# Inverses of the softmax sums: exp(-ln) on ScalarE and one Newton step on VectorE in place of VectorE's reciprocal

## The chip, the core and the metric

The kernel runs on one core of a Trainium2 chip. The metric is the device time of one execution in microseconds (us), the median of several runs. TensorE (PE) multiplies matrices, VectorE (DVE) and ScalarE (ACT) work elementwise, GpSimd (POOL) does masks, some sums and indirect DMAs, and SyncE (SP) issues most other DMAs. Each engine takes its instructions in a fixed order; between engines, semaphores say when a result is there.

## What is computed

Two transformer layers on a tensor of 8 batches of 512 tokens by 512 features, all in float32. Each of the four steps is followed by a layer norm:

```python
x = layernorm(x + attention0(x))     # 16 heads of 32, causal softmax
x = layernorm(x + experts(x))        # top 2 of 8 experts with low-rank adapters
x = layernorm(attention1(x))         # RMS-scaled input, 8 heads of 64, 2 key/value heads, adds x itself
x = layernorm(x + integer_ffn(x))    # weights given as integers and a scale for each row
```

In both attentions a head's output is softmax(scores) times the values. The kernel computes exp(scores) without subtracting a maximum, multiplies by the values, sums the exponentials of each query, and multiplies the product by the inverse of that sum. The change concerns this inverse.

## The kernel before

`usual_pass` runs four stages one after the other: attention 0 (0 to about 690 us), the expert tiles (to about 1060 us), attention 1 (to about 1600 us) and the integer FFN. A guard (`Guard`) gathers the sums of the exponentials and their inverses; if any were out of range, a slower general pass would follow.

**Attention 0** loops over 8 batches `b` and 4 groups `g` of four heads. A group has three units `u` of key tiles, `UNITS = ((0,), (1, 3), (2,))`. `scores` (L1477) lets TensorE fill `sc`, one tile that takes four banks of PSUM, and ScalarE takes the exponential (L1492) into `p`. Where `beside` holds, adapter products also go into `sc`, and ScalarE copies them out as `scaled` (L817) behind that exponential. GpSimd masks the diagonal (L1502). One unit later TensorE multiplies by the values (`av`, L1531), and VectorE adds up the `p` of a group (L1539). At the second unit of the next group, `normalise` (L1542) lets TensorE form the sums with a matrix of ones (`rs`, L1546). ScalarE copies them to `r_inv` and adds them up for the guard (L1081), VectorE takes the reciprocal (L1549) and multiplies (`aoT`, L1550). GpSimd adds the inverse to the guard's total (L1084). The other work of a batch (queries, keys, values, the output projection, the router, transposes `ps_x1T`) is put into slots of `plan` (L1563). TensorE follows the order in which this is written; the other engines' instructions are placed by the scheduler here, until the last groups.

**Attention 1** is written out by hand for TensorE, VectorE, ScalarE and GpSimd (`in_order`, L1805). A batch has 8 steps of two score units each; a group of two heads has four units, so two steps. In each step (L1966 to L1976) come, in order: the scores of two units (`sc`, two tiles of two banks) and their exponentials (L1876), VectorE's additions for the two units of the step before (`total`, L1884), the slot's other work, the products `av` (L1895) of the units of the step before, and every second step the normalisation of the group that is now complete (L1900): `rs` on TensorE (L1903), the copy on ScalarE (L1081), the reciprocal on VectorE (L1906), the product into `aoT` (L1913), and GpSimd's addition for the guard. The slots hold queries (`qT`, L1770), the key, the values, the projection `ps_o` of the batch before with its residual and statistics (L1848, L1856), and the preparation of the next batch (`xn`, L769; transposes L98). `r_inv` and `total` have one buffer each, `p` has four. PSUM outside the scores and `av` is two banks that `rs`, `ps_q`, `ps_k`, `ps_v` and `ps_o` take in turn.

ScalarE evaluates functions from a table that it has to load. Loads are put into the program when it is built. Before the change they stand at the first activation (L1404), around the router's exponential and the experts' Silu (L973, L526, L973), at the start of attention 1 (L1828, in `prepare_table(AF.Exp)`) and at its end (L1828, for Silu).

Of the kernel before, what the change touches and what calls it, by code (L numbers as in the profile page):

```python
# [9 lines left out]
F32 = mybir.dt.float32  # L10
# [3 lines left out]
AF = mybir.ActivationFunctionType  # L14
ALU = mybir.AluOpType
# [3 lines left out]
P = 128  # L19
NB = 8  # L20
S = 512
D = 512
NT = S // P
ND = D // P
# [26 lines left out]

SUM_LOW, SUM_HIGH = 1e-20, 1e20

WIDEST = 2048.0


# [11 lines left out]
def in_order(tc, *engines):  # L68


    return tc.manual_schedule(engines={mybir.EngineType.PE, *engines})


class Inputs:
# [40 lines left out]
class Env:  # L115
# [19 lines left out]
    def open_stream(self, ctx, batches, **kw):  # L135

        resident = ctx.enter_context(self.tc.tile_pool(name=f"resident{batches[0]}", bufs=1, **kw))
        for b in batches:
            self.xs[b] = resident.tile([P, NT, D], F32, tag=f"x{b}", name=f"x_{b}")
# [919 lines left out]
class Guard:  # L1059
# [26 lines left out]
    def partitions_held(self, const, ps):  # L1086
# [3 lines left out]
        nc.vector.tensor_reduce(red[:, 3:4], self.widest[:, : self.n_widest], AX.X, ALU.max)  # L1090
        nc.vector.tensor_scalar(red[:, 3:4], red[:, 3:4], WIDEST, None, ALU.is_le)
        nc.vector.tensor_reduce(red[:, 0:1], self.total, AX.X, ALU.add)
# [61 lines left out]
class IntegerFfn:  # L1154
# [102 lines left out]
    def batch(self, b):  # L1257
        env, nc = self.env, self.nc
        os = [self.p_o.tile([P, D], F32, tag=f"o{t}", name=f"ps_f{t}") for t in range(NT)]
        final = b == NB - 1  # L1260
        hold = NHID - self.HELD if final else NHID
        parts = {}
        for c in range(NHID):
            parts[c] = self.hidden(b, c, c >= hold)
            if 0 < c <= hold:
                for t in range(NT):
                    self.out(os, t, c - 1, parts[c - 1])

            if not final and c < NT:
                self.blocks(b + 1, c)  # L1270
            if not final and 0 <= c - 6 < ND:
                self.parts(b + 1, c - 6)
        if not final:
            for t in range(NT):
                self.out(os, t, NHID - 1, parts[NHID - 1])
            for t in range(NT):
                self.scaled(b, os, t)
            env.layernorm(b, lambda t: env.ins.out[b][ts(t, P), :])
            return

        with in_order(env.tc, mybir.EngineType.DVE, mybir.EngineType.Activation, mybir.EngineType.Pool):
            for t in range(NT):
                for c in range(hold, NHID):
                    self.out(os, t, c, parts[c])
                self.last_rows(b, t, self.scaled(b, os, t))
# [22 lines left out]
def attention0(env, guard, keep, routes, experts, dram, p_mm, tiles_ctx):  # L1308
# [4 lines left out]
    tc, nc, ins, xs, vec = env.tc, env.nc, env.ins, env.xs, env.vec  # L1313
    HD = 32
    scale = 1.0 / math.sqrt(HD)
    UNITS = ((0,), (1, 3), (2,))
    with ExitStack() as phase:
        work = phase.enter_context(tc.tile_pool(name="a_work", bufs=1))
# [4 lines left out]
        p_av = heads_ctx.enter_context(tc.tile_pool(name="a_av", bufs=2, space=PSUM))  # L1323


        wv, wq, wk, wo = (experts.room(i) for i in (0, 2, 3, 5))

        def load_w(room, i, units=slice(0, ND)):
# [45 lines left out]
        def mm(shape, name):  # L1374
            return p_mm.tile(shape, F32, tag="mm", name=name)
# [166 lines left out]
        def normalise(b, g, acc):  # L1542
            total, av = acc
            rs = p_av.tile([P, S], F32, tag="av", name="rs") if (b, g) == (NB - 1, ND - 1) else mm([P, S], "rs")
            for j in range(4):
                nc.tensor.matmul(rs[HD * j : HD * (j + 1), :], lhsT=ones, rhs=total[:, j, :], start=True, stop=True)  # L1546
            r_inv = work.tile([P, S], F32, tag="r_inv", name="r_inv", bufs=2)
            guard.watch_sums(rs, r_inv)
            nc.vector.reciprocal(r_inv, r_inv)  # L1549
            normed[0] = nc.vector.tensor_tensor(aoTs[b][:, g, :], av, r_inv, ALU.mult)  # L1550
            if (b, g) == (NB - 1, ND - 1):
                guard.watch_inverses(r_inv)
            else:
                inverses.append(r_inv)
# [65 lines left out]

        begun = phase.enter_context(ExitStack())
        begun.enter_context(in_order(tc))
        query(0, 0)
        key(0, 0)
        order = phase.enter_context(ExitStack())
        waiting = summing = None
        for b in range(NB):
            todo, late = plan(b)
            for g in range(ND):
                if g == (0 if b else 2) and b + 1 < NB:  # L1630
                    with behind_return():
                        load_xT(b + 1)
                if g == 3 and b + 1 < NB:
                    with behind_return():
                        load_x(b + 1)
                if b == NB // 2 and g == 0:
                    experts.load_lora(work, 1)
                if b == NB - 1 and g == 1:
                    experts.load(4)
                if b == NB - 1 and g == 2:  # L1640
                    order.enter_context(in_order(tc))
                if b == NB - 1 and g == 3:
                    experts.load(5)
                    experts.load(6)
                acc = []
                for u in range(len(UNITS)):
                    p = scores(b, g, u)
                    for thunk in todo[g, u]:
                        thunk()
                    begun.close()  # L1650
                    if waiting is not None:
                        waiting()
                    for thunk in late[g, u]:
                        thunk()
                    if u == 1 and summing is not None:
                        summing()
                    waiting = lambda b=b, g=g, u=u, p=p, acc=acc: product(b, g, u, p, acc)
                summing = lambda b=b, g=g, acc=acc: normalise(b, g, acc)
# [6 lines left out]
        b = NB - 1  # L1665
# [28 lines left out]
class Attention1:  # L1694
# [113 lines left out]
    def batches(self, work, p_sc, p_av, weights, split):  # L1808
        env, nc, guard, state, HD = self.env, self.nc, self.guard, self.state, self.HD
        xs = env.xs  # L1810
        scale = 1.0 / math.sqrt(HD)
# [14 lines left out]
        def prepare_table(function):  # L1826
            out = work.tile([P, 2, S], F32, tag="p", name="p1_none", bufs=4)
            nc.scalar.activation(out[:, 0, :1], env.neg_half[:, :1], function)  # L1828

        prepare_table(AF.Exp)  # L1830

        small = env.small
        pieces = {0: self.first}
# [35 lines left out]
        def score(b, g, kt):  # L1869
            st = state[b]  # L1870
            sc = p_sc.tile([P, 2, S], F32, tag="sc", name="sc1")
            for j in range(2):
                hs = slice(HD * j, HD * (j + 1))
                matmul_by_columns(nc, sc[:, j, :], st["kT"][hs, ts(kt, P)], st["qT"][g][hs, :], columns=HD)
            p = work.tile([P, 2, S], F32, tag="p", name="p1", bufs=4)
            nc.scalar.activation(p, sc, AF.Exp, scale=scale)  # L1876
            return p
# [10 lines left out]
        def product(b, g, kt, p):  # L1888
            st = state[b]
            if b and (g, kt) == (0, 0):  # L1890
                st["aoT"] = work.tile([P, ND, S], F32, tag="aoT", name="aoT1", bufs=2)
            if kt == 0:
                st["av"] = p_av.tile([P, S], F32, tag="av", name="av1")
            for j in range(2):
                nc.tensor.matmul(st["av"][HD * j : HD * (j + 1), :], lhsT=st["v"][:, kt, HD * j : HD * (j + 1)],  # L1895
                                 rhs=p[:, j, :], start=kt == 0, stop=kt == NT - 1)
            if kt == NT - 1:
                return lambda total=st["total"], av=st["av"]: normalise(b, g, total, av)

        def normalise(b, g, total, av):  # L1900
            rs = self.mm([P, S], "rs1")
            for j in range(2):
                nc.tensor.matmul(rs[HD * j : HD * (j + 1), :], lhsT=ones, rhs=total[:, j, :], start=True, stop=True)  # L1903
            r_inv = work.tile([P, S], F32, tag="r_inv", name="r_inv1")
            guard.watch_sums(rs, r_inv)
            nc.vector.reciprocal(r_inv, r_inv)  # L1906
            ao = state[b]["aoT"][:, g, :]
            if b != self.BY_TENSOR:

                ao, av, r_inv_ = self.turn.by_tile(ao, False), self.turn.by_tile(av, True), self.turn.by_tile(r_inv, True)  # L1910
            else:
                r_inv_ = r_inv
            nc.vector.tensor_tensor(ao, av, r_inv_, ALU.mult)  # L1913
            guard.watch_inverses(r_inv)
# [50 lines left out]
        for b in range(NB):  # L1965
            for i, thunks in enumerate(plan(b)):  # L1966
                units = [(b, u // NT, u % NT) for u in (2 * i, 2 * i + 1)]
                ps = [score(*unit) for unit in units]
# [4 lines left out]
                sums = [product(*unit) for unit in last]  # L1973
# [5 lines left out]
        sums = [product(*unit) for unit in last]  # L1979

        b = NB - 1
# [368 lines left out]
```

## Time and profile before

| | |
|---|---|
| median of 3 runs | 2098.43 us (2098.05 to 2098.45) |
| the profiled execution | 2098.14 us |
| its span, first to last instruction | 2096.2 us |
| mean granted TensorE clock | 0.999 |
| ScalarE copies of sums (L1081) | 64, mean 597 ns |
| reciprocals, attention 0 (L1549) | 32, 107.0 us |
| reciprocals, attention 1 (L1906) | 32, 107.1 us |
| table loads seen on ScalarE | 6, mean 1283 ns |

In the profile, a line such as `L1906 DVE RECIPROCAL r_inv<-r_inv ... x32 | 107.1, 3347 | 72.7 <-ACT r_inv L1081 72.7` names the line of code, the engine, the operation, output and input, how many, the busy us, the mean ns of one, then the idle us of the engine just before them and who ended it. A row of a time line has the start in us, the duration in us, engine, line, operation and count; in square brackets stands the idle time before it and who ended it. PEld is the loading of weights into TensorE. The ends of matmuls are modelled, and a busy TensorE is not necessarily one at its peak.

### The profile page before, as it was taken

What the parts mean: (1) busy time and instruction counts of PE and PEld (TensorE: products, weight loads), DVE (VectorE), ACT (ScalarE), POOL (GpSimd) and SP (SyncE); (2) the same over time, 40 slices, a digit from 0 to 9 for tenths busy, and PEclk for the clock granted to TensorE, in tenths of its full rate; (3) what the DMA queues carried; (4) which work ended last, traced back from release to release, by engine and by line L of the source; (5) the groups of instructions that cost most, each with busy time, mean ns of one, the idle gap of its engine ahead of it and who ended that gap; (6) DMA issues with size and microseconds to landing.
All of it is one profiled execution on the core that took longest, in us unless ns stands there. A gap on an engine that the chain in (4) does not pass through costs nothing. (4 is left out here: it accounts for less than half of the span.)

```text
span 2096.2 us, 35861 instructions
## 1 busy us (share of the span) xinstructions
PE 2072.5 (99%) x15074; PEld 1048.4 (50%) x15074; DVE 1275.9 (61%) x1965; ACT 606.8 (29%) x840; POOL 503.3 (24%) x509
## 2 busy tenths in 40 slices
PE   9999999999999999999999999999999999999998
PEld 2333333333334677774433333333335888888886
DVE  2667776777768633234157888887868644455444
ACT  2333433324333111111143333333332322222222
POOL 1343444434433221221052231222101000000000
PEclk9999999999999999999999999999999999999999
DMA  9011304324233568876431332233102311111000
GB/s 327 22 46 57 102 16 117 122 70 154 82 102 112 171 200 256 243 225 203 148 101 51 121 111 81 66 106 101 41 1 71 101 41 61 61 61 61 20 21 22
DMA packets 182090, 213.39 MB, mean 102 GB/s; under 512 B 72586, under 2 KB 126090, under 8 KB 178850
## 3 DMA queue, kind: packets, MB, share of 16 engines
q1 hardware_dynamic: 169280, 172.85, 26.3%
q0 software_dynamic: 10560, 34.61, 5.7%
q10 hardware_dynamic: 2082, 3.56, 0.6%
q8 instruction: 121, 1.98, 0.4%
q14 instruction: 47, 0.39, 0.1%
HBM read 132.58 MB, written 78.40 MB: 101 GB/s over the span
## 5 line engine op out<-in xcount | busy, mean ns | idle before, releaser
L1492 ACT ACTIVATE p<-sc 128x2048 f32<-128x2048 f32 (+1 forms) x96 | 153.1, 1595 | 172.0 <-PE sc L65 148.3
L1236 DVE SCALAR_TENSOR_TENSOR hT<-ps_u,vec,sg 128x512 f32<-128x512 f32 x88 | 65.5, 745 | 190.1 <-PE ps_u L1231 189.9
L1084 POOL TENSOR_TENSOR g_total<-g_total,r_inv 128x512 f32<-128x512 f32 x64 | 90.7, 1417 | 351.8 <-DVE r_inv L1906 270.8
L1247 PE MATMUL ps_f<-ffn_w,h_half 128*128 128x512 f32 x664 | 167.7, 393 | 2.7 <-DVE h_half L1242 2.0
L964 PE MATMUL ps_gu<-xrT,experts 128*128 128x256 f32 x736 | 166.6, 379 | 0.0
L964 PEld LDWEIGHTS ps_gu<-xrT,experts 128*128 128x128 f32 x736 | 139.3, 190 | 35.9 <-issue 19.3
L1539 DVE TENSOR_TENSOR p<-p 128x1536 f32<-128x1536 f32 (+2 forms) x96 | 136.5, 1422 | 32.6 <-PE av L1531 17.6
L1502 POOL TENSOR_SCALAR_AFFINE_SELECT p<-p 128x512 f32<-128x512 f32 x128 | 84.4, 672 | 290.7 <-ACT p L1492 287.6
L1876 ACT ACTIVATE p<-sc 128x1024 f32<-128x1024 f32 x128 | 124.2, 1022 | 100.3 <-PE sc L65 99.0
L1906 DVE RECIPROCAL r_inv<-r_inv 128x512 f32<-128x512 f32 x32 | 107.1, 3347 | 72.7 <-ACT r_inv L1081 72.7
L1247 PEld LDWEIGHTS ps_f<-ffn_w,h_half 128*128 128x128 f32 x664 | 122.9, 188 | 34.4 <-DVE h_half L1242 7.3
L1231 PE MATMUL ps_g<-x_high,ffn_w 128*128 128x512 f32 x352 | 137.2, 390 | 0.0
L1231 PE MATMUL ps_g<-x_low,ffn_w 128*128 128x512 f32 x352 | 137.0, 389 | 0.0
L1231 PE MATMUL ps_u<-x_high,ffn_w 128*128 128x512 f32 x352 | 137.0, 389 | 0.0
L1231 PE MATMUL ps_u<-x_low,ffn_w 128*128 128x512 f32 x352 | 137.0, 389 | 0.0
L65 PE MATMUL sc<-qT,kT 64*64 64x512 f32 x1024 | 124.7, 602 | 1.2 <-ACT qT L1770 0.9
L65 PE MATMUL ps_q<-experts 128*32 128x512 f32 x1024 | 121.2, 602 | 4.7 <-DMA experts<-in_xT 4.4
L65 PE MATMUL ps_v<-experts 128*32 128x512 f32 x1024 | 120.9, 594 | 0.0
L1895 PE MATMUL av<-p,v 128*64 128x512 f32 x512 | 120.8, 593 | 0.0
L1234 ACT ACTIVATE sg<-ps_g,vec 128x512 f32<-128x512 f32 x88 | 60.6, 689 | 195.4 <-PE ps_g L1231 195.4
L65 PE MATMUL ps_o<-attn_out,aoT 128*64 128x512 f32 x512 | 116.4, 598 | 0.0
L65 PE MATMUL ps_k<-experts 128*32 128x512 f32 x1024 | 116.3, 594 | 0.0
(280 smaller groups left out, 3270.3 us busy)
## 6 DMA issues: line engine op xcount, KB each, us to landing
results<-y SPq DMA_DIRECT2D x68, 256.0 KB, 2.9
pair<-xrT SPq DMA_DIRECT2D x30, 512.0 KB, 3.0
xrT<-pair SPq DMA_DIRECT2D x120, 128.0 KB, 3.9
turned<-turned SPq DMA_DIRECT2D x56, 256.0 KB, 4.1
x<-in_x SPq DMA_DIRECT2D x8, 1024.0 KB, 8.5
rows<-x SPq DMA_DIRECT2D x32, 256.0 KB, 2.1
experts<-in_xT SPq DMA_DIRECT2D x7, 1024.0 KB, 11.8
x<-rows SPq DMA_DIRECT2D x14, 512.0 KB, 6.6
```

Of the source, the lines that this page charges most:

```text
L65: nc.tensor.matmul(out[m], lhsT=lhsT[:, m], rhs=rhs, start=start, stop=stop)
L964: nc.tensor.matmul(ps[:, j, :], lhsT=w, rhs=xT[:, c, :], start=c == 0, stop=c == ND - 1)
L1084: self.nc.gpsimd.tensor_tensor(self.total, self.total, r_inv, ALU.add)
L1231: nc.tensor.matmul(ps, lhsT=w[:, ts(dc, P)], rhs=x[:, dc, :], start=(dc, i) == (0, 0), stop=(dc, i) == (ND - 1, 1))
L1236: nc.vector.scalar_tensor_tensor(hT, u, vec[:, V_SU + c : V_SU + c + 1], sg, ALU.mult, ALU.mult)
L1247: self.nc.tensor.matmul(os[t], lhsT=h[:, ts(t, P)], rhs=self.weights(2 * NHID + c), start=(c, i) == (0, 0), stop=(c, i) == (NHID - 1, 1))
L1492: nc.scalar.activation(p, sc[:, :, :width], AF.Exp, scale=scale)
L1502: select = nc.gpsimd.affine_select(out=first, in_=first, pattern=[[0, 4], [1, P]], compare_op=ALU.is_ge, fill=0.0, base=0, channel_multipl ...
L1539: nc.vector.tensor_tensor(total[:, :, P * kt :], total[:, :, P * kt :], p[:, :, at : at + w], ALU.add)
L1876: nc.scalar.activation(p, sc, AF.Exp, scale=scale)
L1895: nc.tensor.matmul(st["av"][HD * j : HD * (j + 1), :], lhsT=st["v"][:, kt, HD * j : HD * (j + 1)], rhs=p[:, j, :], start=kt == 0, stop=kt ...
L1906: nc.vector.reciprocal(r_inv, r_inv)
```

## The change

Of the 64 inverses, 63 are made by a new function; the last one of attention 0 keeps its reciprocal. ScalarE takes ln of the sums straight from PSUM, then exp of minus that; VectorE makes one Newton step of it, with `sums` the copy that the guard's line makes: (2 - sums * rough) * rough. In attention 0 `rough` takes a buffer of the tag `r_inv`, which has two; in attention 1 it has one of its own. At the start of attention 0 and of attention 1 a table set that holds both functions is asked for; in attention 1 this stands in place of the activation that prepared Exp.

```diff
+EXP_AND_LN = "natural_log_exp_and_others"
...
+def inverse(nc, sums, ps, rough):
+
+    nc.scalar.activation(rough, ps, AF.Ln)
+    nc.scalar.activation(rough, rough, AF.Exp, scale=-1.0)
+    nc.vector.scalar_tensor_tensor(sums, sums, -1.0, rough, ALU.mult, ALU.mult)
+    nc.vector.scalar_tensor_tensor(sums, sums, 2.0, rough, ALU.add, ALU.mult)
...
+        nc.scalar.preload_act_table_set(EXP_AND_LN)
         wv, wq, wk, wo = (experts.room(i) for i in (0, 2, 3, 5))
...
             guard.watch_sums(rs, r_inv)
-            nc.vector.reciprocal(r_inv, r_inv)
+            if (b, g) == (NB - 1, ND - 1):
+                nc.vector.reciprocal(r_inv, r_inv)
+            else:
+                inverse(nc, r_inv, rs, work.tile([P, S], F32, tag="r_inv", name="r_rough", bufs=2))
...
-        prepare_table(AF.Exp)
+        nc.scalar.preload_act_table_set(EXP_AND_LN)
...
             guard.watch_sums(rs, r_inv)
-            nc.vector.reciprocal(r_inv, r_inv)
+            inverse(nc, r_inv, rs, work.tile([P, S], F32, tag="r_rough", name="r_rough1"))
```

In the changed kernel's numbering the preloads are L1336 and L1844, Ln and Exp of the inverse L78 and L79.

## Prediction, made before the changed kernel was run

> **What bounds the kernel now.** I read the page's busy shares first, then the waits of TensorE in the two stretches that hold the attentions, then time lines around a normalisation. The page:
>
> ```profile
> PE 2072.5 (99%) x15074; PEld 1048.4 (50%) x15074; DVE 1275.9 (61%) x1965; ACT 606.8 (29%) x840; POOL 503.3 (24%) x509
> ...
> L1906 DVE RECIPROCAL r_inv<-r_inv 128x512 f32<-128x512 f32 x32 | 107.1, 3347 | 72.7 <-ACT r_inv L1081 72.7
> ```
>
> TensorE is busy for all but 23.7 us of the span. 64 reciprocals cost VectorE 214 us, but VectorE is not what the span is made of. Waits of TensorE in 40 to 700 us (attention 0); each row is us in total, times, longest:
>
> ```profile
> PE sc L65 <- ACT p L1492: 1.2, 1, 1.2
> PE ps_x1T L1443 <- DVE r_table L603: 0.7, 1, 0.7
> ```
>
> And in 1055 to 1610 us (attention 1), the longest:
>
> ```profile
> PE sc L65 <- ACT qT L1770: 0.9, 1, 0.9
> ```
>
> All of TensorE's waits in attention 0 come to 2.8 us, in attention 1 to 3.4. So the gain is capped at some 6 us even if every wait there vanished, and most are not behind a reciprocal. What matters is the slack of the new chain. The place to read is a normalisation in attention 1 and the next row sum (time line of a middle batch, VectorE, TensorE and weight loads):
>
> ```profile
> 1189.65 1.89 PE L1895 MATMUL av<-p,v 128*64 128x512 f32 x8
> ...
> 1190.93 0.14 PEld L1903 LDWEIGHTS rs<-total,ones 128*64 128x64 f32 x2 [0.28 <-issue]
> ...
> 1193.22 3.35 DVE L1906 RECIPROCAL r_inv<-r_inv 128x512 f32<-128x512 f32 x1 [5.44 <-ACT r_inv L1081]
> ...
> 1196.68 0.69 DVE L1913 TENSOR_TENSOR aoT<-av,r_inv 128x512 f32<-128x512 f32 x1
> ...
> 1197.28 1.73 DVE L1884 TENSOR_TENSOR total<-p,p 128x1024 f32<-128x1024 f32 x1
> ...
> 1203.71 2.52 DVE L1884 TENSOR_TENSOR total<-total,p 128x1024 f32<-128x1024 f32 x2
> ...
> 1204.86 1.89 PE L1895 MATMUL av<-p,v 128*64 128x512 f32 x8
> ...
> 1206.35 0.38 PEld L1903 LDWEIGHTS rs<-total,ones 128*64 128x64 f32 x4 [0.48 <-issue]
> 1206.58 1.03 PE L1903 MATMUL rs<-total,ones 128*64 128x512 f32 x4
> ```
>
> The first reciprocal begins only when ScalarE's copy of the sums ends (VectorE had sat idle 5.44 us), and from its end VectorE works without a gap to 1206.23, when the next group's total is ready. The next row sum loads its weights 0.12 us later, 1.49 us after its av began, where the undisturbed distance is 1.28 (1189.65 to 1190.93). So that total is already just in time: TensorE has no slack there, though no wait is printed. The same place recurs every 67.8 us.
>
> **What the change removes and adds.** Per inverse it removes a 3.35 us reciprocal and adds on VectorE two scalar_tensor_tensor of 128x512. Nearest row: L735, 741 ns, in pairs 1.53 us; L1254's plain two-operand form at 684 is the lower end. I take 1.53. On ScalarE it adds Ln and Exp of 128x512, nearest row L1081, 597 ns. Saved on VectorE 1.8 us, 63 times, 115 us; added on ScalarE 1.2 us, 76 us. Both engines have room, so neither sum is a time.
>
> The instruction order of the built program shows more. TensorE, GpSimd and SyncE keep their orders; no DMA moves. In attention 0 ScalarE has one table load at its start (L1336) and none before the expert tiles. In attention 1 the preload of L1844 leaves no instruction. A load stands before the first score exp (where L1828's stood) and **one ahead of every Ln and one ahead of every Exp of the inverse, 64 in all**. What one costs, from ScalarE's time line in the expert tiles:
>
> ```profile
> 721.21 0.60 ACT L973 ACTIVATE h<-ps_gu 128x512 f32<-128x512 f32 x1 [2.98 <-PE ps_gu L964]
> 721.83 1.28 ACT L526 ACT_TABLE_LOAD   x1
> 723.12 0.23 ACT L526 ACTIVATE tmp<-tmp 128x32 f32<-128x32 f32 x1
> ```
>
> End of one activation to start of the next: 1.31 us, nothing hidden around the load. The Trainium skill, "ScalarE: Activation LUTs", section "What ACT_TABLE_LOAD costs", gives about 1283 ns for the load, which agrees, and adds about 1380 ns of drain, 2.66 us for every switch. It speaks against this change; the row shows no drain, and I take 1.31. By the page the chain below would be 2.7 us longer (first rival). Its section "Table sets" says Ln and Exp share a set and need one load; the built program in attention 1 does not do that.
>
> **Attention 1.** From the end of ScalarE's copy, C: before, reciprocal at C+0.04, 3.35, 0.11 to the product, 0.69: aoT done at C+4.19. After: load 1.31, Ln 0.60, load 1.31, Exp 0.60 = C+3.82, two vector steps with their gaps 1.69, product 0.69: C+6.2. So **aoT is 2.0 us later; I take 1.95**, with 1.8 to 2.0 from the two vector prices. Queued behind the waiting vector step are aoT, the next adds, residuals and statistics; behind ScalarE's chain the two score exps of the next step. VectorE's saving can't pay this back where VectorE was waiting for the copy anyway.
>
> Against it, place by place (end of the last add to the weight load of the row sum, less 0.12 latency, plus what a late weight load hides, about 0.2):
> - Normalisation in a batch's first step, next total (1138, 1206, 1274, 1342, 1410, 1477 us): slack nil. 6 x 1.95 = 11.7.
> - The next one: VectorE reaches the reciprocal 1.7 us after the copy, so C+3.82 exceeds its arrival by only about 2.1 while 1.8 of work are saved: 0.35 late, slack 0.33. Nothing.
> - The third (five batches): slack 1.25-0.12+0.2 = 1.34. 5 x 0.6 = 3.0.
> - The fourth: slack 6.3. Nothing.
> - Batch 0: row sum at 1086.47, its total ended 1086.42: 1.95. Transposes at 1096.54, xn ended 1096.44: 1.9.
> - Batch 7: slack 1.7 at 1574.88: 0.25. Slack 0.3 at 1587.21: 1.65.
> - Entry of the integer FFN: its first matmul at 1599.81 follows the third residual (ended 1599.76); VectorE is then 1.3 later than TensorE: 1.3.
>
> Sum 21.8. The score exps come 3.8 us later: at 1261 the first ends at 1265.8 instead of 1262.3, its bank is wanted at 1267.29, 1.5 us spare. The qT copies of batch 0 end some 0.2 late, inside the waits already counted. The final aoT comes at 1595.6, its matmuls at 1596.2.
>
> **Attention 0.** No loads, so the chain is C+1.2+1.7+0.69 against 4.19: shorter, and VectorE is often behind anyway. ScalarE's third exp of a group slips by about 0.75 us. Where logits follow, the bank is close:
>
> ```profile
> 331.93 1.08 ACT L817 ACTIVATE scaled<-sc 128x512 f32<-128x512 f32 x2
> ...
> 333.53 1.11 PE L65 MATMUL sc<-q,k 32*64 32x512 f32 x16
> ```
>
> scaled would end at 333.75 instead of 333.01: 0.3 us, 6 batches, 1.8. In other groups the bank is wanted over 1 us after. Of the 0.7 us wait for r_table at 644, which lies behind a reciprocal, I credit all: -0.7. Bounds -2.8 to +4; I take +1.1.
>
> **Sum.** 21.8 + 1.1 = 22.9 on the profiled execution's 2098.14 us (span 2096.2 and 1.9 around it): 2121.0. The median of the runs is 0.29 higher: 2121.3.
>
> **The rivals.**
> 1. The load costs 2.66 us as the page says. aoT is then 4.65 late; places 1 to 3 of a batch cost 4.65, 2.7 and 3.3, batch 0 9.3, the end 12: about 83 us, 2181. Against it: the time line above. 5 in 100.
> 2. VectorE's lateness shrinks on its way. The first add after aoT takes 1.73 us beside GpSimd's g_total, the same shape later 1.26; if that add falls free and the vector steps take 684 ns, the delay is about 1.3: 6 x 1.3, 0 for the third place, 2.6 in batch 0, 1.6 at the end, and attention 0 gives 0.5 back: 2110. For it: the two durations; against: g_total starts when r_inv is ready, so it moves along. 14 in 100.
> 3. **Not slower:** ScalarE loads a table while still waiting or computing, so that loads stay off the chain. The chain is C+3.6, 0.6 shorter than now; only the capped wait remains to be won: 2097.5. It decides where a load costs under some 0.34 us on the chain (1.31 less half of 1.95). Against it: Ln's load stands after the copy that waits, in order, and the row shows 1.31 between activations. 7 in 100. That the change doesn't do what it says is shown in part already by the 64 loads.
> 4. The score exps also stall TensorE: if the chain exceeds the 1.5 us spare by 0.5 in half the groups, 8 us more: 2132. 6 in 100.
>
> **How the numbers follow.** The likeliest case has 68 in 100 and its own range 2114 to 2128 (delay 1.8 to 2.05, attention 0 from -2 to +4). The range reaches to rivals 2 and 4: 2108 to 2133, some 83 in 100. About 0.2%, 4 us, is what a measurement of this kernel tells from no change. Slower: cases 1, 2, 4 and the likeliest, 0.92; within 0.2% 0.06; faster 0.02, since the cap is 6 us.
>
> **What would show it.** In attention 1 two table loads of 1.28 us per inverse, aoT about 6.2 us after the copy's end; TensorE waits of about 1.95 us at rs <- DVE total, six times, and 0.6 five times; GpSimd waiting longer for r_inv. In attention 0 no loads, VectorE's busy time down by 57 us. The span should grow in 1060 to 1610 and hardly in 40 to 700. It is wrong if a load has a gap around it, if rs shows no wait, or if attention 0 grows by over 4 us.

## The result, and the profile after

The changed kernel takes 2121.14 us (median of 4 runs, 2120.95 to 2121.2), the kernel before beside it 2098.44 (2098.05 to 2098.79): ratio 1.0108, 95% interval 1.0091 to 1.0126. It is 22.7 us slower. The profiled execution has a span of 2119.4 us, 23.2 more than before.

The page after, busy times and the first vector step of the inverse:

```profile
PE 2078.7 (98%) x15074; PEld 1048.2 (49%) x15074; DVE 1170.3 (55%) x2028; ACT 753.4 (36%) x1029; POOL 507.3 (24%) x509
...
L80 DVE SCALAR_TENSOR_TENSOR r_inv<-r_inv,r_rough 128x512 f32<-128x512 f32 x63 | 44.0, 698 | 160.2 <-ACT r_rough L79 160.0
```

VectorE is busy 105.6 us less than before, and yet the kernel is slower. At 47 of the 63 inverses VectorE now sits idle until ScalarE's `r_rough` is there, 160 us in all; before, it sat idle 72.7 us for the copies of the sums. TensorE's longest waits in 1055 to 1640 us (us in total, times, longest):

```profile
PE rs L1917 <- DVE total L1898: 15.8, 13, 2.5
PE ps_g L1241 <- DVE x L1862: 1.0, 1, 1.0
```

Neither row stands in the list of before. The time line of the place that the prediction showed (a batch's first normalisation, ScalarE and VectorE, and the next row sum):

```profile
1201.47 0.60 ACT L1091 ACTIVATE r_inv<-rs 128x512 f32<-128x512 f32 x1 [2.05 <-PE rs L1917]
1201.97 0.19 ACT L1091 ACTIVATION_READ_ACCUMULATOR r_inv<-rs 128x1 f32 x1
1202.18 1.28 ACT L78 ACT_TABLE_LOAD   x1
1203.47 0.60 ACT L78 ACTIVATE r_rough<-rs 128x512 f32<-128x512 f32 x1
1204.09 1.28 ACT L79 ACT_TABLE_LOAD   x1
1205.38 0.63 ACT L79 ACTIVATE r_rough<-r_rough 128x512 f32<-128x512 f32 x1
1205.92 1.92 ACT L1890 ACTIVATE p<-sc 128x1024 f32<-128x1024 f32 x2
...
1206.12 0.69 DVE L80 SCALAR_TENSOR_TENSOR r_inv<-r_inv,r_rough 128x512 f32<-128x512 f32 x1 [6.23 <-ACT r_rough L79]
...
1207.64 0.69 DVE L1927 TENSOR_TENSOR aoT<-av,r_inv 128x512 f32<-128x512 f32 x1
...
1208.25 1.79 DVE L1898 TENSOR_TENSOR total<-p,p 128x1024 f32<-128x1024 f32 x1
...
1217.40 1.08 PE L1917 MATMUL rs<-total,ones 128*64 128x512 f32 x4 [1.68 <-DVE total L1898]
```

The copy ends, with its accumulator read, at 1202.16; `aoT` is done at 1208.33, 6.17 us later (4.19 before). From `aoT` on VectorE has no gap until the next total, and the row sum, just in time before, now waits 1.68 us.

To see where the time came from, I set the start of each group of TensorE's products in the profile after against the start of the same group before. The shift grows in the steps below. Steps of up to 0.1 us are left out, and so is one of 0.76 us at 74.86 us, which is gone again at the next group.

| place (time before) | step, us |
|---|---|
| keys' first product, 9.65 us | 1.20 |
| six score groups behind logits, 165 to 586 us | 6 x 0.21 |
| `ps_x1T` at 645.88, first scores of attention 1 at 1061.47 | -0.18, -0.18 |
| batch 0: `rs` at 1086.47, scores at 1087.48, `ps_q` at 1089.36 | 2.65, 0.25, 1.39 |
| `rs` at 1138.79 and every 67.8 us, six times | 1.85 to 1.86 each |
| `rs` at 1172.65 and every 67.8 us, five times | 0.52 to 0.53 each |
| `rs` at 1575.31 and 1587.64, entry of the integer FFN at 1599.81 | 0.14, 1.55, 1.04 |

About 21 us arise in attention 1, about 2 before it. The theory to test: the two table loads on each chain make VectorE late, and the adds queued behind that wait make the row sum late. Rivals: attention 0 carries a good part; the added activations and vector steps cost by themselves; the loads hold up the score exponentials; a load costs more than its 1.28 us.

### The profile page after: what moved, and what is told of

It reads as the page before. It is cut to its first block, busy times and chain, and to the rows that moved or that the text cites. A ratio compares the mean times of both kernels' runs of the same rounds, so it can differ in the third digit from the quotient of the medians.

```text
span 2119.4 us, 36153 instructions
## 1 busy us (share of the span) xinstructions
PE 2078.7 (98%) x15074; PEld 1048.2 (49%) x15074; DVE 1170.3 (55%) x2028; ACT 753.4 (36%) x1029; POOL 507.3 (24%) x509
## 5 line engine op out<-in xcount | busy, mean ns | idle before, releaser
L1513 POOL TENSOR_SCALAR_AFFINE_SELECT p<-p 128x512 f32<-128x512 f32 x128 | 98.6, 782 | 339.6 <-ACT p L1503 337.0
L1550 DVE TENSOR_TENSOR p<-p 128x1536 f32<-128x1536 f32 (+2 forms) x96 | 144.3, 1503 | 37.5 <-POOL x L1523 31.4
L80 DVE SCALAR_TENSOR_TENSOR r_inv<-r_inv,r_rough 128x512 f32<-128x512 f32 x63 | 44.0, 698 | 160.2 <-ACT r_rough L79 160.0
L1091 ACT ACTIVATE r_inv<-rs 128x512 f32<-128x512 f32 x64 | 38.2, 597 | 244.2 <-PE rs L1917 119.7
```

The source lines that it names most:

```text
L1513: select = nc.gpsimd.affine_select(out=first, in_=first, pattern=[[0, 4], [1, P]], compare_op=ALU.is_ge, fill=0.0, base=0, channel_multipl ...
L1550: nc.vector.tensor_tensor(total[:, :, P * kt :], total[:, :, P * kt :], p[:, :, at : at + w], ALU.add)
```

## Experiments: which attention, and which part of the chain

**Attention 0 alone.** Attention 1 as before (`prepare_table(AF.Exp)`, `nc.vector.reciprocal`).

> Only attention 0 takes the new inverse; attention 1 keeps VectorE's reciprocal and its own preparation of Exp. My theory: nothing in attention 0 loads a table, the inverse is off TensorE's path, and only ScalarE's later third exponentials reach TensorE where logits follow (6 x 0.21 us in the trace after), against some 0.35 gained at waits; with the 1.2 us that the trace after shows at its first key product, if that belongs to the table load asked for at the start, 2100.5 us; without it 2099.3. Rival, that the two extra ScalarE activations and the changed order in attention 0 cost a good part of the 22.7 us: over 2105.

2099.32 us; before 2098.24; ratio 1.0006 (0.9997 to 1.0015). The six steps of 0.21 us are there. But the keys' first product starts 0.44 us *earlier* than before, with the same early load.

**Attention 1 alone.** Attention 0 as before.

> Only attention 1 takes the new inverse, with its 64 table loads; attention 0 is as before. My theory: all of the loss but some 2 us lies here, by an aoT that comes 1.9 to 2 us late: 2119.5 us (2118.5 to 2121). Rival, that attention 0 carries a good part of it: under 2115.

2119.65 us, ratio 1.0103 (1.0087 to 1.0118): 21.4 of the 22.7 us. The trace also shows where attention 1's request for the shared set went. L1840 is that request's line in this kernel:

```profile
1.25 1.28 ACT L1840 ACT_TABLE_LOAD   x1 [1.25 <-PEq L2350]
```

It was carried out 1.25 us after the program's start, some 1060 us before attention 1. Before attention 1 begins, three other loads follow it, for the router and the experts (at 667.96, 721.50 and 729.31 us). In the full change the load at 1.25 us stands at attention 0's request, and none is seen at attention 1's.

**One set.** The whole change with one line kept:

```diff
+        prepare_table(AF.Exp)
         nc.scalar.preload_act_table_set(EXP_AND_LN)
```

> The whole change, but in attention 1 the activation that prepares Exp stays and the shared set is asked for after it: in the built program the shared set is then loaded once there, and the 64 loads before Ln and Exp are gone; nothing else in the inverse differs. My theory (the loads make the chain late): the chain is 3.6 us from the copy's end to aoT instead of 6.2 (4.2 before), TensorE never waits for it, and what is left is attention 0's: 2099.5 us (2098 to 2100.5). Rival, that Ln, Exp and the two vector steps themselves, or ScalarE's fuller queue, are what costs: over 2110.

2100.22 us, ratio 1.0007 (0.9998 to 1.0016). The same place in its time line:

```profile
1195.87 0.19 ACT L1091 ACTIVATION_READ_ACCUMULATOR r_inv<-rs 128x1 f32 x1
1195.96 0.59 ACT L78 ACTIVATE r_rough<-rs 128x512 f32<-128x512 f32 x1
1196.58 0.63 ACT L79 ACTIVATE r_rough<-r_rough 128x512 f32<-128x512 f32 x1
...
1198.84 0.69 DVE L1928 TENSOR_TENSOR aoT<-av,r_inv 128x512 f32<-128x512 f32 x1
```

With one load of the shared set ahead of the stage (its group has one entry, 1.3 us), `aoT` is done 3.47 us after the copy, and none of the steps at 1138 to 1478 us is left; of batch 0's steps 0.42 us remain. The 21 us are the 64 loads, not Ln, Exp or the Newton step.

**One set, attention 1 alone.** As above, attention 0 as before.

> As the run before, but attention 0 as before the change. My theory: attention 1 can only win what it waits for, 3.4 us at most, and hardly any of these waits is behind a reciprocal: 2097.5 us (2096 to 2098.5), a little faster than the kernel before or the same. Rival as in the run before: over 2108.

2099.10 us, ratio 1.0004 (0.9995 to 1.0013): not the small gain that I thought likely. A chain 0.7 us shorter than the reciprocal's wins nothing, since TensorE's longest waits in the stage are the same as before (`sc` on `qT` 0.9, `ps_hT` 0.7), and none is behind an inverse. One short wait is even new: 0.3 us at batch 0's row sum. There the first inverse's two vector steps took 0.98 and 1.06 us, with GpSimd at work beside them, instead of 0.69 each.

**Loads kept, Newton step left out.** In this run and in all the others below, up to the gathers behind, attention 0 is as before the change.

```diff
-            inverse(nc, r_inv, rs, ...)
+            r_inv = work.tile([P, S], F32, tag="r_rough", name="r_rough1")
+            nc.scalar.activation(r_inv, rs, AF.Ln)
+            nc.scalar.activation(r_inv, r_inv, AF.Exp, scale=-1.0)
```

> Attention 1 alone, with its 64 table loads, but the Newton step is left out: exp(-ln) itself is multiplied with av. aoT then ends at the copy's end + 3.85 + 0.04 + 0.69 = 4.6 us instead of 6.2 (before: 4.2). My theory (what counts is by how much aoT is late): 0.4 late, six places of a batch's first step 6 x 0.3, batch 0 and the end 0.3 to 0.5 each, the third place nothing: 2101.5 us (2100 to 2104). Rival (each load costs by itself, some 0.3 us for each of 64): 2117 or more.

2099.95 us against 2098.70, ratio 1.0005 (0.9996 to 1.0015), just under the range that I expected. There are six steps of 0.26 us at the six places and nothing elsewhere in attention 1, not in batch 0 and not at the end either. With sixty-four loads the loss is about 1.3 us, and the interval holds none at all: what counts is by how much the chain is longer than before (4.57 us from copy to `aoT` instead of 4.19), not how many loads there are.

**Copies in the loads' place.** The shared set is loaded once, as in the one-set runs.

```diff
     nc.scalar.activation(rough, ps, AF.Ln)
+    for _ in range(4):
+        nc.scalar.activation(rough, rough, AF.Copy)
     nc.scalar.activation(rough, rough, AF.Exp, scale=-1.0)
```

> Attention 1 alone with the shared set, so no loads, but four copies of rough to itself (ScalarE, 128x512, about 0.62 us each with the gap) between Ln and Exp: 2.5 us in the place of the 2.6 that two loads took. My theory (a load costs as any other work of its length on this chain): nearly the same time as with the loads, 2118.5 us (2116.5 to 2120). Rival (there is something about table loads, such as a drain or their fetch, beyond their 1.28 us): under 2110.

2119.40 us, ratio 1.0096 (1.0079 to 1.0112). Its longest wait of TensorE:

```profile
PE rs L1916 <- DVE total L1897: 15.5, 13, 2.6
```

This is the pattern of the loads without the loads: 13 waits, steps of 1.80 at the six places (1.85 with loads), 0.47 at four of the five and 0.76 at the other. On this chain a load costs what any other 1.28 us of ScalarE would.

**Loads behind the chain.** Shared set, and two needless loads after each Exp.

```diff
     nc.scalar.activation(rough, rough, AF.Exp, scale=-1.0)
+    nc.scalar.preload_act_table_set("exp_and_others")
+    nc.scalar.preload_act_table_set(EXP_AND_LN)
```

> Attention 1 alone with the shared set, and behind each inverse's Exp two loads that nothing needs (Exp's own set, then the shared one again): 64 loads as in the changed kernel, but behind the chain to aoT and ahead of the next step's score exponentials. My theory (VectorE's lateness is what costs, the score exponentials have 1.5 us to spare): 2099.5 us (2098.5 to 2102). Rival (the loads hold up the score exponentials and through them TensorE): over 2110.

```profile
1193.22 0.19 ACT L1093 ACTIVATION_READ_ACCUMULATOR r_inv<-rs 128x1 f32 x1
...
1193.94 0.63 ACT L79 ACTIVATE r_rough<-r_rough 128x512 f32<-128x512 f32 x1
1194.59 1.28 ACT L80 ACT_TABLE_LOAD   x1
1194.68 0.69 DVE L82 SCALAR_TENSOR_TENSOR r_inv<-r_inv,r_rough 128x512 f32<-128x512 f32 x1 [7.45 <-ACT r_rough L79]
...
1195.87 1.28 ACT L81 ACT_TABLE_LOAD   x1
1196.20 0.69 DVE L1926 TENSOR_TENSOR aoT<-av,r_inv 128x512 f32<-128x512 f32 x1
...
1197.17 1.94 ACT L1889 ACTIVATE p<-sc 128x1024 f32<-128x1024 f32 x2
```

2098.38 us against 2098.70, ratio 0.9998 (0.9988 to 1.0007). There are as many loads as in the changed kernel, beside VectorE's steps instead of ahead of them, and nothing is lost. The score exponentials start behind both loads, 3.76 us after the copy as in the changed kernel, and hold nobody up.

## Experiments: who is held up

**Adds first.** Loads on the chain as in the changed kernel, but VectorE's Newton step and product come after the next step's add.

```diff
                 for unit in last:
                     add(*unit)
+                if rest is not None:
+                    rest()
+                    rest = None
                 for thunk in thunks:
                     thunk()
...
-                    sums[-1]()
+                    rest = sums[-1]()
```

(`rest` holds the two vector steps, the product and GpSimd's addition.)

> Attention 1 alone with all its 64 loads in their places, but VectorE's three steps of an inverse (Newton step and the product into aoT) stand behind the first add of the next step instead of ahead of it; ScalarE, TensorE as in the changed attention 1. My theory (aoT itself is wanted much later; what costs is the add queued behind the wait): the add of 1.3 to 1.7 us now fills most of the 1.95 us by which VectorE waited longer, leaving 0.2 to 0.7 us at six places and some in batch 0: 2103.5 us (2099 to 2108). Rival (aoT's or av's own lateness is what TensorE meets): over 2115.

2105.12 us against 2098.70, ratio 1.0029 (1.0018 to 1.0041); its longest wait of TensorE:

```profile
PE rs L1913 <- DVE total L1894: 4.1, 7, 1.2
```

The six steps fall from 1.85 to 0.64, the five vanish, batch 0 costs 1.35. With the same 64 loads, less than a third of the loss is left (6.4 of 21.4 us): TensorE was not waiting for `aoT` but for the add queued behind it.

**The slot's work first, too.** `rest` behind the slot's other work (`for thunk in thunks`) as well.

> As the run with the adds first (attention 1 alone, all 64 loads on the chain), but VectorE's three steps of an inverse stand behind the slot's own VectorE work as well. My theory (the loss is what is queued on VectorE behind the wait, nothing else): VectorE hardly waits for the inverse, the 0.64 us at six places go too, 2099.5 us (2098 to 2102). Rival (aoT late by now some 4 us or the work pushed into the step of the next total is what TensorE meets instead): over 2104.

2122.34 us (2118.66 to 2129.41; before 2099.02), ratio 1.0106 (1.0089 to 1.0123): my expectation failed. The cause is not where the rival put it:

```profile
PE ps_v L67 <- issue: 11.6, 25, 1.0
PE sc L67 <- ACT qT L1780: 3.5, 2, 2.8
PE rs L1913 <- DVE total L1894: 1.3, 1, 1.3
```

The row sums wait once, but in five batches the values' products (`ps_v`) take some 7 us instead of 3.5. They stand still for up to 1 us at a time, and the profile names nothing that they wait for:

```profile
1184.83 0.69 DVE L1923 SCALAR_TENSOR_TENSOR r_inv<-r_inv,r_rough 128x512 f32<-128x512 f32 x1 [1.13 <-ACT r_rough L1918]
1185.17 0.44 PE L67 MATMUL ps_v<-attn_qkv,hT 128*64 128x128 f32 x4 [0.27 <-issue]
1185.46 0.94 POOL L738 DMA_INDIRECT yr<-results,r_results_i  x1 [0.30 <-issue]
1185.55 0.69 DVE L1924 SCALAR_TENSOR_TENSOR r_inv<-r_inv,r_rough 128x512 f32<-128x512 f32 x1
1185.88 0.49 PE L67 MATMUL ps_v<-attn_qkv,hT 128*64 128x128 f32 x5 [0.27 <-issue]
1186.28 0.69 DVE L1930 TENSOR_TENSOR aoT<-av,r_inv 128x512 f32<-128x512 f32 x1
...
1187.36 0.42 PE L67 MATMUL ps_v<-attn_qkv,hT 128*64 128x128 f32 x3 [0.99 <-issue]
```

In this order GpSimd's gathers of later rows (`yr`, L738), which used to stand behind its wait for the inverse, start at 1176.6 us and run beside `ps_v` (1181.9 to 1189.3). The profiled execution is the slowest of the four (2129.41 us). It also lost 2.8 us in batch 0, where scores waited for a copy of `qT`, and the granted clock read 0.50 three times in attention 1, for 3.41, 6.83 and 3.41 us.

**Gathers behind again.** As the last, with these gathers put back behind `rest`.

> As the run with the slot's work first, but in a batch's last step GpSimd's eight gathers of the batch after next stand behind the inverse's GpSimd addition again, as in the kernel before; VectorE's order and the 64 loads stay as in that run. In that run the gathers, no longer held up by that addition, began ahead of the values' products and beside them (1176.6 us; 1183.6 with the adds first), and these products took 7 us instead of 3.4 in each batch. My theory: that overlap is all that was lost there, and with it gone neither the row sums nor the values' products lose time: 2099.5 us (2098 to 2102). Rival (late aoT or VectorE's new order costs by itself): over 2110.

2102.35 us against 2098.61, ratio 1.0018 (1.0009 to 1.0027), just over the range that I expected:

```profile
PE rs L1913 <- DVE total L1894: 2.5, 2, 1.3
PE ps_g L1241 <- DVE x L1858: 1.1, 1, 1.1
```

With 64 loads on the chain, all eleven repeated steps are gone, and `ps_v` takes 3.5 us. The shift grows only by 1.38 in batch 0 and by 1.43 and 1.10 at the end, which I had not put into the expectation: 3.9 us, the measured 3.7.

**Gathers ahead, nothing else.** The kernel before, `fetch` moved from `todo[7]` to `todo[6]`.

> The kernel before with nothing changed but the eight gathers of the batch after next, which GpSimd issues one step earlier, ahead of the addition that waits for the inverse; the inverse is VectorE's reciprocal. My theory of the overlap (the values' products lose 3.5 us a batch where the gathers run beside them): five to six batches lose up to 3.5 us each, 2112 us (2105 to 2122). Rival (the gathers beside them were chance, the loss lay in the order of VectorE): 2098.4 us.

2099.09 us against 2098.61, ratio 1.0002 (0.9993 to 1.0011): my theory of the overlap failed. The gathers ran beside `ps_v` (1168.8 to 1178.7 beside 1175.6 to 1179.1), and it took 3.5 us as ever.

In most places of the failed run a load of integer weights was under way as well (512 KB, issued at 1182.5 us in the place shown). The DMA engines' share from 1181.9 to 1189.3 us was 0.85; with gathers alone it was 0.74 (here, 1175.5 to 1179.1), with weights alone 0.54 (in the run with the gathers behind, 1177.2 to 1180.8). But both at once is not the cause either. In the last of the five slow batches of that run, at 1472.4 us, no weights were on their way (the last such load of the stage was issued at 1401.5), the share was only 0.71, and `ps_v` took 7 us all the same.

What the five have in common is that the first three standstills begin 0.04 to 0.14 us after the start of VectorE's three steps of the inverse, as in the rows above, with gathers under way. The first of these steps beside `ps_v` without gathers stopped nothing (gathers behind), nor did gathers beside a reciprocal and a product into `aoT` (this run). Gathers together with these steps would fit, but that was not tried by itself, and the later standstills of a batch begin at no such step. What TensorE waited for there stays open.

**The wait in batch 0 filled.** In the changed kernel TensorE's longest wait for a row sum, 2.53 us, is followed by slow scores:

```profile
1091.39 1.32 PE L1917 MATMUL rs<-total,ones 128*64 128x512 f32 x4 [2.53 <-DVE total L1898]
...
1092.64 3.34 PE L67 MATMUL sc<-qT,kT 64*64 64x512 f32 x16
```

These scores take 1.95 us elsewhere. The granted clock reads 0.50 in 1092.1 to 1095.5 us, the only such stretch of the stage. I put four products on TensorE ahead of that row sum:

```diff
             rs = self.mm([P, S], "rs1")
+            if (b, g) == (0, 1):
+                for _ in range(4):
+                    nc.tensor.matmul(rs[:HD, :], lhsT=ones, rhs=self.w_qkv[:, 0, :], start=True, stop=True)
```

> The changed kernel with four products of ones with a weight that is there already (their result is written over by the row sums that follow) put on TensorE ahead of batch 0's second row sum, which waits 2.53 us for the total: about 2 us of that wait are now filled. My theory (after this longest wait of the stage TensorE runs at half clock for 3.4 us, and 1.4 us of batch 0's cost are that, no wait): the row sum starts when it did, the scores behind it take 1.95 us again instead of 3.34, no half clock is recorded there, 2119.7 us. Rival (the slow scores belong to the late exponentials or banks, not to the clock): 2121.1 us, or more if the products delay what follows.

2123.59 us (2120.7 to 2124.57; before 2099.02): not faster than the changed kernel, as I had expected it to be. The scores behind it run at full speed again (1.95 us), but the four products took 3.8 us, more than the wait, and half clock came 13 us later:

```profile
1104.98 1.94 PE L1745 MATMUL ps_hT<-ident,xn 128*128 128x128 f32 x8 [0.24 <-ACT hT L1746]
```

These transposes take 1.15 us in the changed kernel; here the granted clock reads 0.50 in 1105.1 to 1108.5 us. So the slow scores were the clock's doing, as I thought, but filling the wait moved the slow stretch and did not remove it. In the 3.41 us ahead of it TensorE was busy 0.88 us in the changed kernel and 2.28 here, while after 1214.98 us of the changed kernel 1.73 busy us of 3.41 brought no half clock. How much idleness it takes is not settled by these runs.

## Why the prediction was right, point by point

- **What bounds the kernel, and the cap.** Right. Even a chain shorter than the reciprocal's wins nothing (2099.10 against 2098.24). Of the 3.4 us that the cap counts for attention 1, 0.5 belong to the expert tiles (`ps_y`) and 0.8 to the integer FFN (`ps_f`).
- **64 loads at 1.31 us each, `aoT` 6.2 us after the copy.** Right: 6.17, hence 1.98 late where I took 1.95. Between the activations a load leaves gaps of 0.01 to 0.02 us; the drain that the Trainium skill states ("ScalarE: Activation LUTs", "What ACT_TABLE_LOAD costs") is not seen, and the first rival (2181) falls.
- **First normalisation of a batch, six times 1.95.** Right: 1.85, 11.1 us for 11.7. Its reason holds too: where the delay was 0.4 the step was 0.26, and with the adds taken out from behind the wait 0.64.
- **The third, five times 0.6.** Right: 0.52 to 0.53 in the table, 2.6 us for 3.0.
- **Batch 0, 1.95 + 1.9.** Size near (4.3), one term wrong. The transposes at 1096.54 lost nothing: the row sum 10 us earlier had put TensorE behind already, and I counted the same lateness twice. In its place came a row sum later than the chain explains (2.65; the two vector steps of the first inverse took 1.20 and 1.06 us, not 0.69, and `aoT` was done 6.95 us after the copy, not 6.17) and 1.39 us of half clock, which the prediction did not have.
- **Batch 7 and the entry of the FFN, 0.25 + 1.65 + 1.3.** The order is right; they measured 0.14, 1.55 and 1.04.
- **Attention 0, +1.1.** With attention 0 alone 2099.32 against 2098.24, 1.1, though the interval holds no change too. The six places are right, 0.21 each instead of 0.3; the credit of 0.7 at `r_table` was not paid (that wait is still 0.7), only 0.18 twice. VectorE's busy time there fell by 44 us (468 to 424), not by 57; the adds of `p` took 7.8 us more than before (136.5 to 144.3).
- **1.2 us at the start**, in no step of the prediction, can't be put down to the change: with the early load the keys' first product came 0.44 us earlier in one run and 1.35 later in another, without it 0.85 later or 0.20 earlier. In the sum this 1.2 us balances terms that I had too large, so part of the total's closeness is luck.
- **The rivals.** VectorE's lateness does not shrink on its way (1.98 us late at `aoT`, six steps of 1.85); the loads are not off the chain (`aoT` at 6.17 us, and 3.47 without them); the score exponentials stall nobody (loads behind the chain: 2098.38).

By differences of medians attention 1 alone gives 21.4 us and attention 0 alone 1.1, together 22.5 of the measured 22.7.

## What to carry to other kernels

Busy time saved on an engine says nothing while that engine waits: cost the chain from the last shared event (here the end of the copy) to the point where the engine is free again, and set the difference against the slack of what is queued behind it. Count table loads in the built program and in the trace, and look where each was carried out: a request for a set may be carried out far from the line where it is written, here some 1060 us ahead of it. A lateness that has pushed TensorE back once is not to be counted again a few us later.

If a chain has to be long, put independent work of the waiting engine ahead of the wait: the order alone took the loss of attention 1 from 21.4 to 3.7 us, with all 64 loads in place. No version tried beats the kernel before, since none of TensorE's waits in attention 1 stood behind an inverse.

## What the hardware showed unexpectedly

A table load cost no more than its 1.28 us, and nothing where ScalarE had time (64 of them, no measurable change). TensorE fell to half clock for 3.4 us once in attention 1 of the changed kernel, after a window in which it was busy for a quarter; the length agrees with the window of 3413 ns that the Trainium skill gives ("TensorE: Matmul & The Clock Gate", "What's actually happening"). But a busy share of two thirds had the same sequel in another run, and one of a half (1.73 of 3.41 us) had not, so a threshold can't be read from here. In the run with the slot's work first it fell three times in attention 1, at 1075.19, 1187.83 and 1262.92 us. These starts are 112.64 and 75.09 us apart, 33 and 22 times 3.413 us, so in that run the clock changed on a fixed beat; whether it matters where in the beat a wait falls was not tried.

And moving VectorE's work moved GpSimd's wait, which released gathers early, and TensorE stood still at products that depend on neither.
